# Counters first, x's own sums next, and the small VectorE steps put one at a time behind its additions

## The chip, the cores and the metric

The kernel runs on one core of a Trainium2 chip. The core has TensorE (PE) for matmuls, VectorE (DVE), ScalarE (ACT), GpSimd (POOL) and SyncE (SP), each working through its own queue of instructions in order, and 16 DMA engines that they share. The metric is the device time of one execution in microseconds (us); lower is better. Everything is computed in 32-bit floats.

## The reference

x has 64 batches of 64 tokens with 256 features; each batch has a type from 0 to 2.

```python
# cond: a shared gated layer and one per type, mixed by a gate on the first token
share  = (gelu(x @ sWi0) * (x @ sWi1)) @ sWo
expert = (gelu(x @ Wi0[type]) * (x @ Wi1[type])) @ Wo[type]
w = softmax(relu(concat([expert[:, 0], share[:, 0]]) @ g0) @ g1)
c = expert * w0 + share * w1
x = x + causal_attention(c)              # 16 heads of 16
# cond2: three shared layers and two experts of the type, mixed by a second gate
s_j = relu(x @ share_wi[j]) @ share_wo[j]                 # j = 0, 1, 2
out_a, out_b = the same with expert_wi/expert_wo[type] and [type + 1]
p = softmax(gate_vecs / 0.1)             # weighs the two experts of each type
h = mix of (out_a, out_b, s_0, s_1, s_2) by gate_vecs, gate_w1, gate_w2
# router: three layers, top 2 of 8 experts, capacity 10 per batch and expert
out = x + mixture_of_experts(h)
```

## The kernel before, in words

The kernel keeps nearly everything in one large on-chip tile called `arena`, cut up by hand-written offsets, so most rows of the profile read `arena<-arena`. PSUM banks carry names: `p1c`, `p6c`, `p7c`, `p5c`, `p4c` and `px` belong to cond's shared layer, `sac` and `sbc` to its down projection, names ending in `t` or `d` to cond2's typed and shared layers, `phb`, `plgb` and `pgwb` to cond2's gate.

The 64 batches are worked in 8 blocks of 8 batches (512 tokens). Each large matmul is done by a seven-product scheme (`strassen`, L197): the weight is cut into four blocks a11 to a22 and the tokens into b11 to b22, with sums s1 to s4 of weight blocks (`sum_columns`, L156, and `sum_weights`, L166) and sums t1 to t4 of token blocks (`token_sums`, L179, called by `column_blocks` for x, and again for the hidden layer). Product p6 needs s2 and t2. VectorE adds the products together (L221, L228, L232, L236, L241) between TensorE's matmuls; TensorE can't refill a PSUM bank until the addition that reads it is done. Before the first product, x must be loaded, turned by TensorE (`turn_x`: `px`), copied out of PSUM (L764 on ScalarE, L766 on VectorE) and summed (`cut_x`), and the shared weights must be loaded and summed.

The layers are lists of items; item n has a first part (up projection) and a second part (down projection), and `pipeline` runs the first part of item n+1 before the second part of item n. `hook(item, f)` puts other work between these. `trickle(steps, n)` queues n further small steps of a generator, and `tick()`, called at three places in each up product and three in most down products, runs one of them. The generators are:

- `sort()`: from the batches' types, the sorted place of each batch (`pos_i`) and what derives from it. Its counters come from `iota` (L424: POOL makes an integer ramp, VectorE casts it to float, L428).
- `units()`: per block, which type most of its batches have, and the two places where types meet; 48 operations on up to 24 or 64 columns per partition, in seven steps of several operations each.
- `combine2(s)`: cond2's gate for one block: some small steps (`hidden`, `logits`, `spread`), then eight multiplies of 128x512 (L1072) and six additions (L1316), one per tick.

`masks`, `attention_masks`, `sorted_rows`, `expert_weights` and `small_loads` are one-off preparations, hooked to early items or to cond2.

The order of instructions on each engine is not the order of the source: a scheduler places an instruction as early as its data dependences and its own estimates allow, so small steps gathered in one place of the source can float ahead of the additions around them. `tc.issue_after(ins)` holds the instructions traced inside its block behind `ins` on the engine of `ins`.

Of the kernel before, what the change touches and what calls it, by code (L numbers as in the profile page):

```python
# [82 lines left out]
def adaln_attn_ffn(ctx: ExitStack, tc: tile.TileContext, a: dict, out: bass.AP):  # L83
# [43 lines left out]

    def run(steps):
        for _ in steps:
            pass  # L130
# [25 lines left out]
    def sum_columns(eng, o, fs):  # L156

        a11, a12, a21, a22, s1, s2, s4 = (
            o[b][:, :, fs] for b in ("a11", "a12", "a21", "a22", "s1", "s2", "s4")
        )  # L160
        eng.tensor_add(s1, a21, a22)
        eng.tensor_sub(s2, s1, a11)
        eng.tensor_sub(a21, a11, a21)
        eng.tensor_sub(s4, a12, s2)
# [14 lines left out]
    def token_sums(eng, eng2, b):  # L179
        b11, b12, b21, b22, t1, t2, t3, t4 = (b[n] for n in BLOCKS)  # L180
        eng.tensor_sub(t1, b12, b11)  # L181
        eng.tensor_sub(t2, b22, t1)  # L182
        eng2.tensor_sub(t3, b22, b12)  # L183
        eng2.tensor_sub(t4, b21, t2)  # L184

    def column_blocks(t, at, sums):

        y = {
            f"b{c + 1}{n + 1}": t[:, c, at + n * HB : at + (n + 1) * HB].unsqueeze(1)
            for c in range(2) for n in range(2)  # L190
        }
        for n in range(4):
            y[f"t{n + 1}"] = sums[:, n : n + 1, :]
        token_sums(nc.gpsimd, nc.gpsimd, y)
        return y

    def strassen(name, lhs, rhs, nk, n, width, c_out, c_done, at_st=AT_ST):  # L197
# [23 lines left out]
        nc.vector.tensor_add(u2, wide(x6), s1)  # L221
# [6 lines left out]
        nc.vector.tensor_add(u3, wide(x7), u2)  # L228
# [3 lines left out]
        nc.vector.tensor_add(c_out("22"), wide(x5), u3)  # L232
# [3 lines left out]
        nc.vector.tensor_add(c_out("12"), wide(x5), u2)  # L236
# [4 lines left out]
        nc.vector.tensor_add(c_out("21"), wide(x4), u3)  # L241
# [6 lines left out]
    def trickle(steps, n):  # L248

        between.extend([lambda: next(steps, None)] * n)  # L250

    def tick():
        if between:
            f = between.pop(0)
            if f:
                f()
# [8 lines left out]
    def layer(name, n, ups, down, blocks_of, hops, part, after, ahead=None, at_st=AT_ST, scale=None):  # L265
# [4 lines left out]
        def item(g):  # L270
            def first():
# [31 lines left out]
                token_sums(nc.vector, nc.gpsimd, hb)  # L303
# [120 lines left out]
    def iota(name, shape, pattern, base=0, mult=0, keep=False):  # L424
        ti = tmp(shape, name + "_i").bitcast(I32)
        nc.gpsimd.iota(ti, pattern=pattern, base=base, channel_multiplier=mult)
        tf = const.tile(list(shape), F32, name=name) if keep else tmp(shape, name)
        nc.vector.tensor_copy(tf, ti)  # L428
        return tf

# [72 lines left out]
    def sort():  # L503
        iota18 = iota("iota18", [P, NB], [[1, NB]])
        iota4 = iota("iota4", [P, NB // GB], [[GB, NB // GB]])
        iota_sb = iota("iota_sb", [1, NSTEP, 2], [[SB, NSTEP], [0, 2]]).rearrange("o m b -> o (m b)")
        bvals = iota("bvals", [NB, P], [[0, P]], base=-int(OOB), mult=1)
# [3 lines left out]
        nc.vector.tensor_scalar(oh, iota18[0:NB, 0:NTYPE], typ, None, ALU.is_equal)  # L511
        yield
# [87 lines left out]
    def units():  # L600
        at_tmp[:] = [AT_XE * 256, AT * 256]
# [9 lines left out]
        place = iota("place", [P, NB], [[1, NB]])  # L611
        begin = iota("begin8", [P, NSB], [[NG, NSB]])
        types = iota("types", shape, [[1, NTYPE], [0, NSB]])
        order = iota("order", shape, [[-NSB, NTYPE], [-1, NSB]], base=NTYPE * NSB)
        end = tmp([P, NTYPE], "end")
        nc.vector.tensor_add(end, first, cnt)
        lo, n = tmp(shape, "lo"), tmp(shape, "n")
        for t, of in ((lo, first), (n, end)):
            nc.vector.tensor_tensor(t, by_type(of), by_block(begin), ALU.subtract)
            nc.vector.tensor_scalar(t, t, 0.0, float(NG), ALU.max, ALU.min)  # L620
        nc.vector.tensor_sub(n, n, lo)
        nc.vector.tensor_tensor(lo, lo, by_block(begin), ALU.add)
        yield
        most = tmp([P, NSB], "most")
        nc.vector.tensor_reduce(most, n.rearrange("p t m -> p m t"), AX.X, ALU.max)

        top = tmp(shape, "top")
        nc.vector.tensor_tensor(top, n, by_block(most), ALU.is_equal)
        K.utype = const.tile([P, NSB + NFIX], F32, name="utype")
# [4 lines left out]
        nc.vector.tensor_scalar(none, top[:, 0, :], -1.0, 1.0, ALU.mult, ALU.add)  # L634
        nc.vector.tensor_mul(main, main, none)
        rest = tmp(shape, "rest")
        nc.vector.tensor_tensor(rest, types, by_block(main), ALU.is_equal)
        yield
        nc.vector.tensor_scalar(rest, rest, -1.0, 1.0, ALU.mult, ALU.add)
        nc.vector.tensor_scalar(top, n, 0.0, None, ALU.is_gt)  # L640
        nc.vector.tensor_mul(rest, rest, top)
        yield
        nc.vector.tensor_mul(order, order, rest)
        head = tmp([P, 1], "head")
        flat = "p t m -> p (t m)"
        nc.vector.tensor_reduce(head, order.rearrange(flat), AX.X, ALU.max)
        sel = tmp(shape, "sel")
        nc.vector.tensor_scalar(sel, order, head, None, ALU.is_equal)
        yield
        nc.vector.tensor_mul(sel, sel, rest)  # L650
        begins, sizes = tmp([P, NFIX], "begins"), tmp([P, NFIX], "sizes")
        src = tmp([P, NB], "src")
        nc.vector.tensor_copy(src, place)
        got, inside, by = tmp(shape, "got"), tmp([P, NB], "inside"), tmp([P, 1], "by")
        for j in range(NFIX):
            if j:
                nc.vector.tensor_sub(sel, rest, sel)
            for o, v in (
                (begins[:, j : j + 1], lo), (sizes[:, j : j + 1], n),
                (K.utype[:, NSB + j : NSB + j + 1], types),  # L660
            ):
                nc.vector.tensor_mul(got, sel, v)
                nc.vector.tensor_reduce(o, got.rearrange(flat), AX.X, ALU.add)
            nc.vector.tensor_scalar(inside, place, begins[:, j : j + 1], None, ALU.is_ge)
            nc.vector.tensor_add(by, begins[:, j : j + 1], sizes[:, j : j + 1])
            nc.vector.scalar_tensor_tensor(inside, place, by, inside, ALU.is_lt, ALU.mult)
            nc.vector.tensor_scalar(
                by, begins[:, j : j + 1], -1.0, float(NB + GB * j), ALU.mult, ALU.add
            )
            nc.vector.scalar_tensor_tensor(src, inside, by, src, ALU.mult, ALU.add)  # L670
        K.utype_i = const.tile([1, NSB + NFIX], I32, name="utype_i")
        nc.vector.tensor_copy(K.utype_i, K.utype[0:1, :])
        yield
        nc.vector.tensor_scalar(begins, begins, float(S), None, ALU.mult)
        K.fix_i = const.tile([1, NFIX], I32, name="fix_i")
        nc.vector.tensor_copy(K.fix_i, begins[0:1, :])
        K.src_i = const.tile([1, NB], I32, name="src_i")
        nc.vector.tensor_copy(K.src_i, src[0:1, :])

    def sorted_rows():  # L680

        pm_i = tmp([P, 1], "pm_i").bitcast(I32)
        for r in (0, 64):
            nc.gpsimd.iota(pm_i[r : r + 64, :], pattern=[[0, 1]], base=0, channel_multiplier=1)
        pm = tmp([P, 1], "pm")
        nc.vector.tensor_copy(pm, pm_i)
# [7 lines left out]
        K.erev = iota("erev", [P, E], [[-1, E]], base=E, keep=True)  # L694

        K.slot0 = iota("slot0", [P, NI], [[PAIR, NI]], base=E * SSL, keep=True)
        K.slot0l = iota("slot0l", [P, NI], [[0, NI]], base=E * PAIR, keep=True)
        for t in (K.slot0, K.slot0l):
            nc.vector.tensor_scalar(t[64:128, :], t[64:128, :], float(CAP), None, ALU.add)
# [69 lines left out]
    def cut_x(s):  # L769
        xblocks[s] = column_blocks(xn_of(s), 0, area(AT_XSUM1, 4, HB))  # L770
# [19 lines left out]

    sorting, unit = sort(), units()
    items = []
    for s in range(NSB):
# [6 lines left out]
        if s == 0:  # L800
            hook(its[0], masks, lambda: trickle(sorting, 12))
            hook(its[1], lambda: run(sorting), lambda: sort_x(0), lambda: sort_x(1))
        elif s + 1 < NSB:
            hook(its[0], lambda s=s: sort_x(s + 1))
# [4 lines left out]
    hook(items[2], sorted_rows, lambda: later.update(b=biases()))  # L809
    hook(items[3], lambda: later["b"]())  # L810
    hook(items[4], lambda: trickle(unit, 20))
    hook(items[6], lambda: run(unit), expert_weights)
    hook(items[4], attention_masks)
# [444 lines left out]
    def cut_x1(s, j):  # L1258
        at = AT_XSUM2F if s == 0 and j == 0 else AT_XSUM2[j]
        xblocks["d", s] = column_blocks(X, s * SB, area(at, 4, HB))  # L1260
# [132 lines left out]
    turned = turn_x(0)  # L1393
    cut_x(0)
    with tc.issue_after(turned.ins):
        for o in up1:
            sum_columns(nc.vector, o, slice(0, F // 4))
    for o in up1:
        sum_columns(nc.gpsimd, o, slice(F // 4, F // 2))
    sum_weights(nc.gpsimd, down1)  # L1400
# [36 lines left out]
    for s in range(NSB):  # L1437
        its = shared2(s, 1)
        if s == 0:
            hook(its[0], lambda: load_share(2), small_loads)  # L1440
# [25 lines left out]
    def y_blocks(s):  # L1466
        summed[s] = column_blocks(X, s * SB, area(AT_YSUM[s > 0], 4, HB))
# [67 lines left out]
    for n, _ in enumerate(router(0)):  # L1535
        if n >= 17 and behind:
            f = behind.pop(0)
            if f:
                f()
# [275 lines left out]
```

## Time and profile before

| what | us |
|---|---|
| median of 3 runs | 2874.35 (2872.74 to 2874.54) |
| profiled execution | 2876.09 |
| its span, first to last instruction | 2874.4 |
| TensorE busy in the span | 2817.2 |
| VectorE busy | 1458.5 |
| GpSimd busy | 876.8 |
| ScalarE busy | 835.9 |
| mean granted TensorE clock | 0.992 of full |

The profiled execution is one more execution than the three of the median. In the profile's rows the first two numbers are start and duration, "x4" is the number of instructions merged, and square brackets give the idle time of the engine before the row and what ended it. A row merged of several instructions has the busy time of all of them. In lists of waits, the numbers are the total, the count and the longest. A 32-bit product of two instructions counts as x4 in the trace.

### The profile page before, as it was taken

Reading aid. Unit: us, or ns where it says so; the run is one execution under the profiler, and the core shown is the slowest. Engines: PE = TensorE matmul, PEld = TensorE weight load, DVE = VectorE, ACT = ScalarE, POOL = GpSimd, SP = SyncE. Lnnn points to the kernel's source line nnn. Section 1 sums busy time; section 2 is a strip of 40 time slices with the busy share of each in tenths; the row PEclk is TensorE's granted clock in tenths of the full one; section 3 lists DMA queues with packets and bytes.
Section 4 is the critical chain, followed back from the end, with each engine's and each line's share of the span. In section 5 each row is a group of like instructions: output and inputs, shape, how many; then the busy total and the mean of one; then the engine's idle time right before and its main releaser. Section 6 shows DMA issues by size and latency. Waiting matters only on the chain.

```text
span 2874.4 us, 38591 instructions
## 1 busy us (share of the span) xinstructions
PE 2817.2 (98%) x14137; PEld 2313.5 (80%) x14137; DVE 1458.5 (51%) x2732; ACT 835.9 (29%) x1503; POOL 876.8 (31%) x890
## 2 busy tenths in 40 slices
PE   6999999999999999999999999999999999999998
PEld 5888887777777778888888888888888888887776
DVE  6766515666666675533545566556543333333443
ACT  2122114444444333212222222222222222221333
POOL 4354201111123355522323222225412233223332
PEclk8999999999999999999999999999999999999999
DMA  2354454333341012432333433334300000012330
GB/s 89 108 172 130 138 178 126 110 111 111 111 140 43 34 37 77 139 96 55 133 132 138 145 123 115 131 122 139 112 15 5 6 6 6 6 37 79 91 95 7
DMA packets 221661, 262.29 MB, mean 91 GB/s; under 512 B 106440, under 2 KB 178976, under 8 KB 221344
## 3 DMA queue, kind: packets, MB, share of 16 engines
q1 hardware_dynamic: 205120, 224.62, 25.3%
q0 software_dynamic: 16128, 34.16, 3.5%
q8 instruction: 112, 1.84, 0.3%
q10 hardware_dynamic: 224, 1.05, 0.1%
q14 instruction: 77, 0.63, 0.1%
HBM read 197.79 MB, written 59.35 MB: 89 GB/s over the span
## 4 chain that ended last, share of the span: by engine, by line
PE 88%; DVE 5%; DMA 3%; issue 2%; SPq 1%; POOL 1%; ACT 0%; POOLq 0%; DVEq 0%; ACTq 0%
PE e L115 6%; PE po L115 5%; PE sad L115 5%; PE p5r L115 5%; PE p1r L115 5%; PE peg L115 4%; PE pel L115 4%; PE sbd L115 4%; PE sat L115 3%; PE p5d L115 3%; PE p1d L115 3%; PE p4r L115 2%; PE p6r L115 2%; PE p7r L115 2%; PE sbt L115 2%; PE p5t L115 2%
## 5 line engine op out<-in xcount | busy, mean ns | idle before, releaser
L183 POOL TENSOR_TENSOR arena<-arena 128x512 f32<-128x512 f32 (+1 forms) x152 | 202.5, 1332 | 663.2 <-DVE arena L181 541.2
L184 POOL TENSOR_TENSOR arena<-arena 128x512 f32<-128x512 f32 (+1 forms) x152 | 177.1, 1166 | 17.9 <-DVE arena L182 14.6
L115 PE MATMUL sad<-arena 128*128 128x256 f32 x768 | 175.7, 380 | 0.0
L115 PE MATMUL e<-arena 128*128 128x256 f32 x704 | 173.3, 386 | 0.0
L115 PE MATMUL po<-arena 128*128 128x256 f32 (+1 forms) x704 | 170.3, 399 | 0.1
L1152 POOL TENSOR_TENSOR arena<-arena,vrest 128x256 f32<-128x256 f32 x32 | 24.9, 780 | 456.9 <-ACT arena L1149 456.9
L115 PEld LDWEIGHTS sad<-arena 128*128 128x128 f32 x768 | 144.6, 191 | 19.2
L115 PEld LDWEIGHTS po<-arena 128*128 128x128 f32 x704 | 132.9, 190 | 28.5 <-issue 11.5
L115 PEld LDWEIGHTS e<-arena 128*128 128x128 f32 x704 | 129.3, 190 | 30.4 <-issue 14.8
L115 PE MATMUL p5r<-arena 128*128 128x256 f32 x640 | 151.2, 383 | 0.0
L115 PE MATMUL p1r<-arena 128*128 128x256 f32 x640 | 150.1, 381 | 0.0
L115 PE MATMUL peg<-arena 128*128 128x256 f32 x576 | 138.3, 381 | 0.0
L115 PEld LDWEIGHTS p5r<-arena 128*128 128x128 f32 x640 | 119.2, 190 | 23.4 <-DVE arena L232 7.8
L115 PEld LDWEIGHTS p1r<-arena 128*128 128x128 f32 x640 | 119.7, 190 | 21.6 <-issue 5.9
L115 PE MATMUL pel<-arena 128*128 128x256 f32 x576 | 136.1, 379 | 0.0
L115 PE MATMUL sbd<-arena 128*128 128x256 f32 x576 | 132.2, 379 | 0.0
L294 ACT ACTIVATE arena<-arena 128x512 f32<-128x512 f32 x144 | 90.7, 630 | 117.1 <-DVE arena L232 91.0
L914 DVE TENSOR_TENSOR arena<-pel,arena 128x512 f32<-128x512 f32 x72 | 49.7, 690 | 147.8 <-PE pel L115 146.5
L1646 POOL DMA_INDIRECT xs<-arena,slot_i x64 | 62.6, 979 | 203.0 <-ACT arena L1642 108.5
L115 PEld LDWEIGHTS peg<-arena 128*128 128x128 f32 x576 | 108.4, 190 | 17.1 <-issue 2.3
L115 PEld LDWEIGHTS pel<-arena 128*128 128x128 f32 x576 | 109.4, 190 | 14.9
L115 PEld LDWEIGHTS sbd<-arena 128*128 128x128 f32 x576 | 109.4, 190 | 14.9
(404 smaller groups left out, 5891.9 us busy)
## 6 DMA issues: line engine op xcount, KB each, us to landing
arena<-in_L_cond_Wi SPq DMA_DIRECT2D x72, 512.0 KB
arena<-sums_i SPq DMA_DIRECT2D x32, 896.0 KB
arena<-sums_o SPq DMA_DIRECT2D x32, 896.0 KB
arena<-in_L_cond_Wo SPq DMA_DIRECT2D x36, 512.0 KB
arena<-in_L_ffn_eW SPq DMA_DIRECT2D x16, 1024.0 KB
spill<-arena SPq DMA_DIRECT2D x24, 512.0 KB
arena<-spill POOLq DMA_DIRECT2D x24, 512.0 KB, 5.9
arena<-arena SPq DMA_DIRECT2D x128, 64.0 KB
```

What stands on the lines that cost most here:

```text
L115: nc.tensor.matmul(o, lhsT=lhsT, rhs=rhs, start=start, stop=stop, skip_group_check=shared_bank)
L183: eng2.tensor_sub(t3, b22, b12)
L184: eng2.tensor_sub(t4, b21, t2)
L294: nc.scalar.activation(c_out(ij), src, AF.Relu)
L914: nc.vector.tensor_mul(h, hidden("i1", "pel"), g)
L1152: nc.gpsimd.tensor_mul(vx, vn, K.vrest.rearrange("p a b d -> p (a b d)"))
L1646: nc.gpsimd.indirect_dma_start(out=to.rearrange("e n w -> (e n) w"), out_offset=bass.IndirectOffsetOnAxis(ap=slot_i[:, n, i : i + 1], axis=0),
```

## The change

All iotas and casts move into one function, `counters()`, which runs first, with `masks()`. The first block's x copies and sums are held behind the last cast, and x's first sums move from GpSimd to VectorE; the first weight sums of the two up weights are split over GpSimd (`up1[0]`) and VectorE (`up1[1]`), in the order in which the products need them. `sort`'s ticks start at the first product instead of after the first item. `units()` yields after each operation (48 steps, 70 ticks from item 4 on). A list `opening` always holds the latest VectorE addition of a product and the latest GpSimd sum; every tick, and the preparations wrapped in `behind(...)`, run inside `behind_opening()`, which ties each of their instructions on those engines behind these. cond2's gate goes through the same `tick()` and so is tied too. `expert_weights` and what is left of `units` move from item 6 to item 13.

```diff
+    opening = []
+
+    def behind_opening():
+        st = ExitStack()
+        for ins in opening:
+            st.enter_context(tc.issue_after(ins))
+        return st
...
-    def column_blocks(t, at, sums):
+    def column_blocks(t, at, sums, eng=nc.gpsimd):
...
-        token_sums(nc.gpsimd, nc.gpsimd, y)
-        return y
+        return y, token_sums(eng, eng, y)[1]
...
         product("p6", x6)
-        nc.vector.tensor_add(u2, wide(x6), s1)
+        opening[0:1] = [nc.vector.tensor_add(u2, wide(x6), s1).ins]
...
     def tick():
         if between:
             f = between.pop(0)
             if f:
-                f()
+                with behind_opening():
+                    f()
...
-                token_sums(nc.vector, nc.gpsimd, hb)
+                opening[:] = token_sums(nc.vector, nc.gpsimd, hb)
...
+    def counters():
+        K.iota18 = iota("iota18", [P, NB], [[1, NB]])
...
     def units():
...
         nc.vector.tensor_add(end, first, cnt)
+        yield
...
     def cut_x(s):
-        xblocks[s] = column_blocks(xn_of(s), 0, area(AT_XSUM1, 4, HB))
+        xblocks[s], last = column_blocks(xn_of(s), 0, area(AT_XSUM1, 4, HB), nc.gpsimd if s else nc.vector)
+        return last
...
+    def behind(f):
+        def later():
+            with behind_opening():
+                f()
+        return later
...
         if s == 0:
-            hook(its[0], masks, lambda: trickle(sorting, 12))
-            hook(its[1], lambda: run(sorting), lambda: sort_x(0), lambda: sort_x(1))
+            hook(its[0], behind(lambda: run(sorting)))
+            hook(its[1], lambda: sort_x(0), lambda: sort_x(1))
...
-    hook(items[2], sorted_rows, lambda: later.update(b=biases()))
+    hook(items[2], behind(sorted_rows), lambda: later.update(b=biases()))
...
-    hook(items[4], lambda: trickle(unit, 20))
-    hook(items[6], lambda: run(unit), expert_weights)
-    hook(items[4], attention_masks)
+    hook(items[4], lambda: trickle(unit, 70))
+    hook(items[13], behind(lambda: run(unit)), behind(expert_weights))
+    hook(items[4], behind(attention_masks))
...
-    turned = turn_x(0)
-    cut_x(0)
+    masks()
+    counters()
+    with tc.issue_after(K.cast.ins):
+        turned = turn_x(0)
     with tc.issue_after(turned.ins):
+        cut = cut_x(0)
+    with tc.issue_after(cut):
+        opening.append(sum_columns(nc.vector, up1[1], slice(0, F // 4)).ins)
+    with tc.issue_after(K.iota.ins):
+        r = sum_columns(nc.gpsimd, up1[0], slice(0, F // 4))
+    with tc.issue_after(r.ins):
         for o in up1:
-            sum_columns(nc.vector, o, slice(0, F // 4))
-    for o in up1:
-        sum_columns(nc.gpsimd, o, slice(F // 4, F // 2))
-    sum_weights(nc.gpsimd, down1)
+            sum_columns(nc.gpsimd, o, slice(F // 4, F // 2))
+        opening.append(sum_columns(nc.gpsimd, down1, slice(0, P)).ins)
+    trickle(sorting, 13)
...
-            hook(its[0], lambda: load_share(2), small_loads)
+            hook(its[0], lambda: load_share(2), behind(small_loads))
```

## The prediction

> **What bounds the kernel now.** I read the page's engine rows first, then TensorE's waits, then the timeline of the places where those waits lie. The page gives the bound:
>
> ```profile
> PE 2817.2 (98%) x14137; PEld 2313.5 (80%) x14137; DVE 1458.5 (51%) x2732; ACT 835.9 (29%) x1503; POOL 876.8 (31%) x890
> ```
>
> TensorE is busy for 2817.2 of 2874.4 us, so only 57 us of idle time, plus time spent at a low clock, can be won at all. TensorE's waits, longest first (us in total, times, longest):
>
> ```profile
> PE p6c L115 <- POOL arena L182: 15.6, 2, 14.7
> PE p5t L115 <- DVE arena L232: 6.1, 8, 0.8
> PE px L762 <- DMA arena<-in_x: 5.3, 1, 5.3
> PE p4t L115 <- DVE arena L221: 4.8, 7, 0.7
> ...
> PE p5c L115 <- DVE arena L232: 1.9, 2, 1.5
> PE p7c L115 <- DVE arena L221: 1.8, 1, 1.8
> PE phb L115 <- issue: 1.0, 2, 0.7
> PE p4c L115 <- DVE arena L556: 0.9, 1, 0.9
> ```
>
> The change touches three of these: one wait of 14.7 us at the start (p6c), waits of 4.6 us in x's second block (p5c, p7c, p4c), and fifteen short ones (p5t, p4t) in cond2's typed layer. The start, from the timeline (start, duration):
>
> ```profile
> 10.55 0.72 POOL L161 TENSOR_TENSOR arena<-arena 128x256 f32<-128x256 f32 x1 [7.77 <-DMA arena<-in_L_cond_sWi]
> ...
> 16.60 0.68 DVE L766 COPY arena<-px 128x512 f32<-128x512 f32 x1
> ...
> 18.29 0.94 DVE L163 TENSOR_TENSOR arena<-arena 128x256 f32<-128x256 f32 x1
> ...
> 22.85 0.72 POOL L182 TENSOR_TENSOR arena<-arena 128x256 f32<-128x256 f32 x1
> ```
>
> VectorE copies the second half of the turned x at 16.60, though TensorE finished it at 7.21: the copy stands behind a counter's cast, whose iota POOL makes only at 15.96, behind weight sums. x's sums, on POOL behind more weight sums, end at 23.6, and p6c starts at 23.62.
>
> **x's second block.** On TensorE:
>
> ```profile
> 64.05 1.10 PE L115 MATMUL p4c<-arena 128*128 128x256 f32 x4 [0.93 <-DVE arena L556]
> 66.62 2.02 PE L115 MATMUL p5c<-arena 128*128 128x256 f32 x4 [1.46 <-DVE arena L232]
> 68.43 1.87 PE L115 MATMUL p1c<-arena 128*128 128x256 f32 x4
> ...
> 88.16 1.13 PE L115 MATMUL p7c<-arena 128*128 128x256 f32 x4 [1.81 <-DVE arena L221]
> ```
>
> Between 57.45 and 67.6, and again from 82.66 to 90.4, VectorE runs the small steps of `sort`, `units` and `expert_weights` nearly in a row, ahead of the additions that TensorE needs.
>
> **cond2's gate.** On VectorE, then TensorE:
>
> ```profile
> 1539.89 2.95 DVE L1072 TENSOR_TENSOR arena<-arena,gwab 128x512 f32<-128x512 f32 x3
> ...
> 1545.78 0.68 DVE L221 TENSOR_TENSOR arena<-p6t,arena 128x512 f32<-128x512 f32 x1
> ```
> ```profile
> 1546.51 1.13 PE L115 MATMUL p4t<-arena 128*128 128x256 f32 x4 [0.68 <-DVE arena L221]
> 1548.91 1.13 PE L115 MATMUL p5t<-arena 128*128 128x256 f32 x4 [0.84 <-DVE arena L232]
> ```
>
> Seven bulk steps of the gate precede the addition at 1545.78; p6t, started at 1542.08, was done by 1543.2. The same pair of waits returns every 80 us, in seven blocks.
>
> **The change, part by part.** Where I speak of the changed program I mean the order of its instructions on each engine.
>
> *Counters and x first.* POOL now makes all iotas in a row. Four took 0.59 us at 1.94, three 0.32, two of one column 0.32: thirteen end near 4, before x lands at 5.24. The casts follow by 4.5, so VectorE copies px at 7.25 to 7.9. x's sums go to VectorE (four of 128x256). POOL's first weight sum now takes the pieces that the first product needs; SP's waits date these: the first piece at 6.7, the second at 7.45, then one each 0.76 us, which meets the sixth at 10.48. So s1 runs on POOL from 7.5, and p6c needs s2 (POOL's second) and t2 (VectorE's third).
>
> Here a rule speaks against the change. The row: POOL and VectorE, both adding SBUF to SBUF, took 0.90 and 0.94 at 18.3 to 20.9, with starts 0.87 apart, where alone they take 0.72 and 0.41. The Trainium skill, "SBUF — State Buffer", section "SBUF: two separate sides", says that a VectorE operation with two SBUF inputs and a GpSimd operation that reads SBUF exclude each other for the whole instruction. By the rule each pair costs 0.41+0.72 = 1.13, and t2 is ready at 8.25+0.41+2x1.13 = 10.9; by the row 8.25+0.41+2x0.87 = 10.4; with no contention 9.2. I take the row: p6c at 10.5, that is 13.1 earlier.
>
> The clock: matmuls at 23.62 to 28.9 start 0.43 apart, later 0.215, so twelve at half clock cost 2.6 us. The Trainium skill, "TensorE: Matmul & The Clock Gate", Part 1, says that TensorE is slow after about 3.4 us of idling and full again after about 3.4 us of work. By the rule the work from 5.27 to 8.96 might open the clock before p6c, saving 2.6; by the row (slow until 28.9) nothing is saved. I take nothing: VectorE's four sums of the second weight end at 11.2+4x0.87 = 14.7, and the addition of p6c, the type's one-hot and p_214 queue behind these, so a faster TensorE would only wait there.
>
> *sort in the first block.* About 40 steps of 0.06 to 0.2 us (some 6 us) now lie between 22 additions of 0.60 to 0.69 (14 us), in some 20 us: VectorE is full there. p6 of the first down product waits for t2 by my walk about 0.9 us. I charge 1.0 (0 to 3; steps with two SBUF inputs under POOL's sums took 0.63 to 1.2 at 58 to 62). pos_i is ready at 34.5 instead of 73.9.
>
> *The second block is freed.* Waits 0.93+1.46+1.81+0.19 = 4.4 us go, and p5c and p1c, at 1.66 instead of 0.86 each after these gaps, give 1.6.
>
> *SP and POOL queues.* SP's sixteen sorted copies of x move from 75-112 to 35-72 (2.3 us each), with the first blocks' spills among them; four expert loads follow, landing near 75.5 as they landed 3.7 us after issue. POOL's order is new: expert sums now stand before x's sums of the third block. They start at 75.5, and with four sums (3.6 us), an issue (0.8) and six more (0.72 each) t2 is ready near 85.2, where p6c wants it at 84.3. The trace shows no such row; a free POOL would cost nothing, loads 3 us later 5. I take 1.5. The 0.94 us wait of the same kind at 182 I leave in.
>
> *units, masks, expert_weights.* The 48 units steps go one per tick, to the tenth following item; each takes 0.06 to 0.2 us. Between the additions L228 and L232 VectorE has 0.26 us free, so most cost nothing; a step held by POOL's port costs about 0.4 us. I charge 1.0 (0 to 3). expert_weights moves to item 13 with its Exp, two table loads of 1.28 us on ACT: their cover is the 28 matmuls of a second half (6 us); nothing. The attention masks (about 4 us of POOL) and small_loads (1.5 us, with one 32 KB load behind a memset on SP) go where POOL idles 6 to 12 us at a stretch.
>
> *The gate singly.* Now two bulk multiplies precede L221, one follows it, one lies between L228 and L232, and three additions come behind the chain. From the rows: p7 done +0.27, L228 0.60, one multiply 0.60, so L232 starts 0.34 late and is done 0.06 after the filler matmul (0.43) between p4t and p5t. Each block saves 0.68+0.84-0.06 = 1.46, seven save 10.2 (4 if the slack is not there, 13 if fewer clock drops follow).
>
> Sum: -13.1 +1.0 -4.4 -1.6 +1.5 +1.0 -10.2 = -25.8. The profiled run took 2876.09 (span 2874.40 and 1.69 around it), 1.74 above the median of the three shown: 2876.09-25.8 = 2850.3, against the median **2848.6**.
>
> **Rivals.**
> - *Gate steps just change their place in the wait* (15%): the multiply between L228 and L232 holds p5t in both products of a block by 0.7 us, so 7x1.4 comes back: 2858. For: 0.34 of lateness is certain. Against: the filler.
> - *The opening stays bound by VectorE* (8%): port and small steps keep additions late, half of 13.1 is lost and the second block gains 3 rather than 6: 2858.
> - *POOL takes over* (4%, slower): expert sums ahead of x's sums hold p6c in each later block. It decides once an expert load lands more than about 3 us after 75.5. To end slower, six blocks must lose 5.3 us each (2.7 of wait, 2.6 of half clock behind it): -25.8+31.5 = +5.7, 2880. Against: in the trace POOL idles 12.5 us before an expert load at 164 and TensorE waits only 0.94 for the sums behind it.
> - *The ties hold nothing back*: excluded, as the order does show the steps spread.
>
> **Numbers.** What a measurement of this kernel can tell from no change is about 0.2%, 5.7 us. The forecast's own spread with its bounds has 69%, the two lesser gains 23%; a half of the POOL case gives no change (4%), the whole slower (4%). So faster 0.92, same 0.04, slower 0.04. The range runs from all good ends of the opening, clock and gate (2837) to both lesser gains together (2864).
>
> **What would show it.** Right: p6c starts near 10.5; no p4c or p7c wait on L221, L556 in the second block; the p4t rows gone and p5t below 1 us; the clock's slice at 66-70 full. Wrong: waits of p6c for POOL L192 (x's sums) over 3 us in later blocks; new p5t waits at twice the number; L230 of the first block later than 16.

## The result, and the profile after

The changed kernel takes 2844.85 us (median of 6 runs, 2842.82 to 2849.77), the kernel before 2874.44 in the same set (2872.74 to 2875.54): ratio 0.990, 95% interval 0.9887 to 0.9913. That is 29.6 us less; 25.8 were forecast (2848.6, range 2837 to 2864). The profiled run took 2843.99 with a span of 2842.3, 32.1 less than the profiled run before. The lines moved down in the file: the additions L221, L228, L232, L236, L241 are now L230, L237, L241, L245, L250; x's sums L181 to L184 are L191 to L194.

The page's engine rows, and TensorE's waits (total, count, longest, in us):

```profile
PE 2807.5 (99%) x14137; PEld 2310.1 (81%) x14137; DVE 1507.9 (53%) x2732; ACT 836.7 (29%) x1503; POOL 889.0 (31%) x890
```
```profile
PE px L811 <- DMA arena<-in_x: 6.1, 1, 6.1
...
PE p5c L115 <- DVE arena L241: 2.5, 4, 1.6
PE p6c L115 <- POOL arena L192: 2.4, 2, 1.5
...
PE p5c L115 <- DVE arena L615: 0.7, 1, 0.7
PE sac L115 <- DVE arena L192: 0.6, 1, 0.6
...
PE p5t L115 <- DVE arena L241: 0.2, 1, 0.2
```

The wait of 14.7 us, the p4t row and the waits p7c and p4c are gone; p5t is down from 6.1 to 0.2. New are p6c behind GpSimd's L192 (twice), p5c behind L241 (four times), and two small ones behind sort (L615, and sac). VectorE is busy for 49 us more with the same 2732 instructions. Most of that lies in the gate's own steps: its 48 additions (L1373) take 1172 ns each instead of 682, 64 of its multiplies (L1129) 1013 instead of 798, because some of them now run beside GpSimd's sums (1.76 at 1535.58, beside L193 from 1535.08 to 1536.79).

The opening, from the timeline (start, duration):

```profile
8.09 0.69 DVE L815 COPY arena<-px 128x512 f32<-128x512 f32 x1 [3.48 <-PE px L811]
...
9.92 0.94 DVE L192 TENSOR_TENSOR arena<-arena 128x256 f32<-128x256 f32 x1
...
11.01 2.04 PE L115 MATMUL p6c<-arena 128*128 128x256 f32 x4 [1.06 <-DVE arena L192]
...
15.11 0.68 DVE L230 TENSOR_TENSOR arena<-p6c,arena 128x512 f32<-128x512 f32 x1
```

VectorE's copy now follows the end of px directly, and t2 (L192) releases p6c at 11.01, after the 1.06 us of waiting that remain. In this run x landed at 6.11 instead of 5.27, which is chance (4.96 to 5.48 in all runs below); so places in the first layer are counted from the first px from here on. The first layer as a whole, from the first px to its last p1c, took 320.2 us before and 304.6 after (304.9 in a second profile).

cond2's gate, one block, TensorE only. The first fence is of the kernel before, the second of the changed one:

```profile
1541.21 1.03 PE L115 MATMUL p1t<-arena 128*128 128x256 f32 x4
...
1544.80 1.03 PE L115 MATMUL p5t<-arena 128*128 128x256 f32 x4
1546.51 1.13 PE L115 MATMUL p4t<-arena 128*128 128x256 f32 x4 [0.68 <-DVE arena L221]
1547.48 0.59 PE L115 MATMUL sat<-arena 128*128 128x256 f32 x2
1548.91 1.13 PE L115 MATMUL p5t<-arena 128*128 128x256 f32 x4 [0.84 <-DVE arena L232]
...
1555.49 0.81 PE L115 MATMUL p1t<-arena 128*128 128x256 f32 x3
```
```profile
1525.85 1.03 PE L115 MATMUL p1t<-arena 128*128 128x256 f32 x4
...
1529.44 1.03 PE L115 MATMUL p5t<-arena 128*128 128x256 f32 x4
1530.31 1.03 PE L115 MATMUL p4t<-arena 128*128 128x256 f32 x4
1531.17 0.59 PE L115 MATMUL sat<-arena 128*128 128x256 f32 x2
1531.60 1.12 PE L115 MATMUL p5t<-arena 128*128 128x256 f32 x4
...
1538.17 0.59 PE L115 MATMUL p1t<-arena 128*128 128x256 f32 x2
```

The item that holds the gate took 14.28 us from p1t to p1t and takes 12.32; no wait is printed. The two matmuls of `sat` between p4t and p5t are the prediction's filler.

### The profile page after: what moved, and what is told of

Same layout as the page of the kernel before. It is cut to its first block, busy times and chain, and to the rows that moved or that the text cites. A ratio compares the mean times of both kernels' runs of the same rounds, so it can differ in the third digit from the quotient of the medians.

```text
span 2842.3 us, 38609 instructions
## 1 busy us (share of the span) xinstructions
PE 2807.5 (99%) x14137; PEld 2310.1 (81%) x14137; DVE 1507.9 (53%) x2732; ACT 836.7 (29%) x1503; POOL 889.0 (31%) x890
## 3 DMA queue, kind: packets, MB, share of 16 engines
q8 instruction: 112, 1.84, 0.3%
## 4 chain that ended last, share of the span: by engine, by line
PE 92%; DVE 3%; issue 2%; DMA 1%; SPq 1%; POOL 1%; ACT 0%; POOLq 0%; DVEq 0%; ACTq 0%
PE e L115 6%; PE sad L115 5%; PE po L115 5%; PE p5r L115 5%; PE p1r L115 5%; PE peg L115 4%; PE pel L115 4%; PE sat L115 4%; PE sbd L115 4%; PE p5d L115 3%; PE sbt L115 3%; PE p1d L115 3%; PE p4r L115 2%; PE p6r L115 2%; PE p7r L115 2%; PE p5t L115 2%
## 5 line engine op out<-in xcount | busy, mean ns | idle before, releaser
L193 POOL TENSOR_TENSOR arena<-arena 128x512 f32<-128x512 f32 (+1 forms) x151 | 203.3, 1347 | 711.9 <-DVE arena L191 568.9
L194 POOL TENSOR_TENSOR arena<-arena 128x512 f32<-128x512 f32 (+1 forms) x151 | 183.4, 1215 | 14.3 <-DVE arena L192 10.4
L115 PEld LDWEIGHTS pel<-arena 128*128 128x128 f32 x576 | 109.4, 190 | 14.9
L115 PEld LDWEIGHTS sbd<-arena 128*128 128x128 f32 x576 | 109.4, 190 | 14.9
```

The lines of the kernel that those rows point to most:

```text
L115: nc.tensor.matmul(o, lhsT=lhsT, rhs=rhs, start=start, stop=stop, skip_group_check=shared_bank)
L194: return r.ins, eng2.tensor_sub(t4, b21, t2).ins
```

## The experiments

All were run beside the kernel before. "First layer" is the distance just defined; "gate stage" goes from the first p1t to the last (604.2 before). The last is the noisier. Two profiles of the changed kernel give 588.1 and 593.7 with nearly the same idle time of TensorE (4.2 and 3.9): behind the waits of phb TensorE's clock falls to half in some blocks and not in others, in three stretches of the first profile and six, one of them longer, of the second. Each distance comes from one profiled run, which can lie some us beside its kernel's median.

| kernel | median us | against before in its set | first layer | gate stage |
|---|---|---|---|---|
| changed | 2844.85 | -29.6 | 304.6 | 588.1 |
| changed, again | 2843.45 | -31.5 | 304.9 | 593.7 |
| gate loose | 2859.39 | -13.3 | 305.4 | 600.8 |
| before + gate ties | 2857.84 | -14.9 | 319.2 | 585.0 |
| opening only | 2861.55 | -11.2 | 305.9 | 603.8 |
| ties for the gate only | 2846.10 | -26.6 | 306.4 | 585.0 |
| opening swapped | 2844.98 | -29.4 | 304.8 | 590.8 |
| x sums ahead | 2845.23 | -29.1 | 302.3 | 588.7 |
| units grouped | 2850.86 | -23.5 | 307.9 | 587.9 |
| masks between | 2848.03 | -26.3 | 307.6 | 587.9 |
| sort late, masks between | 2846.31 | -28.6 | 308.4 | 587.4 |
| sort late | 2848.68 | -26.3 | 312.3 | 590.7 |
| no expert sums | 2843.02 | -31.9 | 301.7 | 588.9 |

The intervals are about 0.16% to either side, 4.7 us; where two of these kernels differ by less, I go by the first layer and by rows.

### The gate alone, taken away and added

First in the changed kernel, where `loose` is set at the gate's first block, then in the kernel before, with `opening` as in the change and `gating` set at the same place:

```diff
...
-                with behind_opening():
+                with nullcontext() if loose else behind_opening():
                     f()
```
```diff
...
-                f()
+                with behind_opening() if gating else nullcontext():
+                    f()
```

> The changed kernel (2844.9) with the ties taken off the steps of cond2's gate alone. Theory as predicted: each of seven blocks gives back the idle time of the rows before, 1.46 us, so 10.2: about 2855, p4t and p5t wait 0.68 and 0.84 again. Second theory, after comparing the traces: what counts is the distance from one start to the next, not the idle time in brackets; from p1t of one product to that of the next there were 14.28 us before and 12.33 after, 1.95 more, so 13.7 for seven, and 1 to 3 for clock drops: 2859 to 2862. Rival: the gate's gain came from other ties (units, preparations) or from the clock: about 2845.

> The kernel before (2874.4) with only the ties of cond2's gate added. By the bracketed waits 10.2 less: 2864. By distances from start to start 13.7 to 16 less: 2858 to 2861. Rival, the gate's additions need the other parts of the change: 2874.

Measured: 13.3 less than before instead of 29.6 with the gate loose, and 14.9 less (ratio 0.995, 0.9933 to 0.9967) with its ties alone. The waits of the loose kernel are those of before:

```profile
PE p5t L115 <- DVE arena L241: 6.1, 8, 0.8
...
PE p4t L115 <- DVE arena L230: 4.8, 7, 0.7
```

So the gate's gain stands by itself and needs no other part, and it is nearer 15 than my 10.2. The size comes from the distances: in the kernel before each of the seven items takes 14.28 from p1t to p1t, with the ties alone 12.31, and 7 x 1.97 = 13.8. (The gate stage is 19.3 shorter in this run; most of the rest is half clock, four stretches behind phb before and one here, and these change from run to run.) The brackets add up to only 0.68+0.84 = 1.52 per item. The rest lies in the starts, in the two fences of the section before: p5t to p4t took 1.71 (0.87 undisturbed), p4t to the filler 0.97 (0.86), the filler to p5t 1.43 (0.43), in all 1.95. A bracket counts from the modelled end of the matmul before, 0.16 too late at each wait, and the restarted product runs 0.11 longer.

### The opening alone

No ties; sort, units and the preparations in the groups and places of before:

```diff
-        for ins in opening:
+        for ins in []:
...
-            hook(its[0], behind(lambda: run(sorting)))
-            hook(its[1], lambda: sort_x(0), lambda: sort_x(1))
+            hook(its[0], lambda: trickle(sorting, 13))
+            hook(its[1], lambda: run(sorting), lambda: sort_x(0), lambda: sort_x(1))
```

> Counters first, x's sums on VectorE and the new order of weight sums, as in the changed kernel; sort, units and the preparations in the groups and places of before, and no tie anywhere. As predicted: p6c at 10.5 to 11, 13 us off the kernel before, the second block's waits (4.6 us in brackets, some 6 with the half clock) stay: about 2861. Rival, the opening stays bound by VectorE, as sort's first steps float in among the additions: half of 13 is lost, 2868.

Measured: 11.2 less (0.9963, 0.9949 to 0.9977), as expected at 2861.55. p6c starts 4.35 us behind the first px (4.90 in the changed kernel, 18.35 before), the first layer takes 305.9: 14.3 of the 15.6 that it gains in all. The second block keeps its stalls:

```profile
50.89 1.10 PE L115 MATMUL p4c<-arena 128*128 128x256 f32 x4 [0.93 <-DVE arena L593]
53.47 1.13 PE L115 MATMUL p5c<-arena 128*128 128x256 f32 x4 [1.48 <-DVE arena L241]
72.88 1.13 PE L115 MATMUL p7c<-arena 128*128 128x256 f32 x4 [1.37 <-DVE arena L230]
```

Behind the first two of them TensorE kept its full clock here (p5c 1.13), where the kernel before fell to half behind 0.93 and 1.46 (p5c 2.02).

So sort, units and ties, which take these stalls away, bring only 1.3 us net in this layer. Where the rest of their gain went is the question of the next runs.

### The ties of the first layer

```diff
...
-        for ins in opening:
+        for ins in opening if gating else []:
```

> The changed kernel with all ties off until cond2's gate; order of tracing, single steps and early start of sort stay. Theory: the ties free the second block; without them steps of sort and units gather ahead of additions again and TensorE waits 4 to 8 us more for VectorE in the first three blocks: 2849 to 2853. Rival: the early start and the single steps are enough: 2845, within 1. Second rival: the ties keep steps out of VectorE's idle time and cost something: 2842.

Measured: 2846.10, between theory and first rival; the first layer is 1.8 longer. Without ties the stalls do return, with the half clock behind them (p1c of 1.91 next):

```profile
52.94 1.10 PE L115 MATMUL p4c<-arena 128*128 128x256 f32 x4 [2.20 <-DVE utype_i L728]
55.41 2.07 PE L115 MATMUL p5c<-arena 128*128 128x256 f32 x4 [1.37 <-DVE arena L241]
```

Five waits in the first two blocks sum to 6.3 us, yet the layer is only 1.8 longer. This kernel has none of the changed kernel's new waits, and its first L230 starts 7.4 behind px instead of 9.0. In sum TensorE idles just as long in this layer, 306.40 - 298.64 = 7.8 us against 304.62 - 296.88 = 7.7; the 1.8 is busy time, most of it from matmuls at half clock behind the stalls. So the ties of the first layer move the waits and save next to nothing of them; that they save half clock rests on this one place. In the two kernels without ties in this layer GpSimd's masks had floated into the opening, and VectorE's sums beside these took 0.41 or 0.42 instead of 0.83 to 0.94.

### Masks put there on purpose

```diff
...
     with tc.issue_after(r.ins):
+        attention_masks()
         for o in up1:
```

> The changed kernel with GpSimd's attention masks (memsets and selects, no sums) put between its first four weight sums and the others, instead of in the second block. In the runs with loose ties the masks stood there by themselves, VectorE's sums beside them took 0.41 us instead of 0.83 to 0.94, and the first addition (L230) ran at 12.7 instead of 15.1. Theory, GpSimd's sums hold VectorE's: L230 at about 13 with x landing at 5.3, the second product's p1c (18.95 there, with x landing 0.84 later) at 16 to 17, 1.5 to 2.5 us less: 2843. Rival: only the slower first addition moves, TensorE waits for the second part of the weight sums, which GpSimd now makes 3 us later (p6c at 26): 2845.

The first half of the theory came true: L230 at 12.22, the second product's p1c at 16.09. But the first layer is 3.0 longer (the median 3.2, within the intervals), in a third way that neither named:

```profile
21.52 0.82 DVE L575 TENSOR_TENSOR arena<-arena 128x1 f32<-128x1 f32 x1
22.29 1.26 POOL L173 TENSOR_TENSOR arena<-arena 128x512 f32<-128x512 f32 x1
...
25.55 0.79 PE L115 MATMUL p5c<-arena 128*128 128x256 f32 x1 [2.77 <-DVE arena L241]
```

GpSimd's sums of the down weight, 128x512, now start 3.6 us later behind px, where sort's small steps stand between VectorE's additions. A step on one column (0.15 in the changed kernel) takes 0.8, three of them 1.70, and p5c waits 2.77. What VectorE wins early it loses to the same GpSimd work a little later.

### Which engine sums x

x's first sums on GpSimd, up1[0]'s first weight sums on VectorE:

```diff
-        xblocks[s], last = column_blocks(xn_of(s), 0, area(AT_XSUM1, 4, HB), nc.gpsimd if s else nc.vector)
+        xblocks[s], last = column_blocks(xn_of(s), 0, area(AT_XSUM1, 4, HB))
...
     with tc.issue_after(turned.ins):
-        cut = cut_x(0)
-    with tc.issue_after(cut):
+        r = sum_columns(nc.vector, up1[0], slice(0, F // 4))
+    with tc.issue_after(r.ins):
         opening.append(sum_columns(nc.vector, up1[1], slice(0, F // 4)).ins)
     with tc.issue_after(K.iota.ins):
-        r = sum_columns(nc.gpsimd, up1[0], slice(0, F // 4))
-    with tc.issue_after(r.ins):
+        cut = cut_x(0)
+    with tc.issue_after(cut):
```

> The changed kernel with x's first sums back on GpSimd, and the first weight sums of up1[0], which GpSimd made, on VectorE ahead of those of up1[1]. If the opening's gain comes from the order (counters ahead, the copy of px early) and not from the engine that sums x: p6c within 1 us of the changed kernel's, taken from the end of px (2.1 after it there), and the time 2844 to 2846. If it comes from x's sums being on VectorE: GpSimd's two sums of 0.7 to 0.9 behind the second copy put p6c 1 to 2 us later, 2846 to 2847.

Measured: 2844.98 and 304.8, the same; p6c 4.50 behind the first px against 4.90. (The 2.1 in that text is the changed kernel's distance from the end of the copy, more exactly 2.2; from the end of px it is 3.0.) The opening's gain is the order, counters and copy ahead; the engine makes no difference that can be measured. What the counters, the copy and the order of the weight sums bring singly was not separated.

### x's sums ahead of the hidden sums

```diff
-                opening[:] = token_sums(nc.vector, nc.gpsimd, hb)
                 if g == n - 1 and ahead:
                     ahead()
+                opening[:] = token_sums(nc.vector, nc.gpsimd, hb)
```

> The changed kernel with the next block's x sums traced ahead of the hidden layer's sums. On GpSimd x's t1 and t2 (L191, L192) then stand ahead of the hidden t3 and t4 (L193, L194, 128x512, 1.3 to 1.8 us each). Theory: the two new waits of p6c for L192, 1.54 and 0.87 us and 0.17 more each from start to start, go: 2.7 less, 2842. Rival: the hidden t3 and t4 come later, and p7 or p4 of the down product waits for them instead, or x's copies on VectorE hold L191 and L192 of the hidden layer: 2845, with a new wait of sac or sbc.

In the changed kernel's second block a hidden sum (L193, 128x512) stands between x's t1 and t2 on GpSimd:

```profile
46.00 1.11 POOL L191 TENSOR_TENSOR arena<-arena 128x256 f32<-128x256 f32 x1 [13.22 <-DVE arena L815]
47.07 1.77 POOL L193 TENSOR_TENSOR arena<-arena 128x512 f32<-128x512 f32 x1
48.81 0.71 POOL L192 TENSOR_TENSOR arena<-arena 128x256 f32<-128x256 f32 x1
...
49.58 1.13 PE L115 MATMUL p6c<-arena 128*128 128x256 f32 x4 [1.54 <-POOL arena L192]
```

With the order turned, that wait is gone and no new wait of sac or sbc stands in its place (sac's 0.6 of the first block is there in both kernels); the second, at 86.56, stays at 0.72. The first layer takes 302.3, 2.3 less. The medians do not show it (2845.23 against 2844.85): it is half of their interval.

### GpSimd's expert sums left out

```diff
-        sum_weights(nc.gpsimd, weight_blocks(t, at + 4))
+        nc.gpsimd.memset(area(at + 4, 3 * 256), 0.0)
```

> The changed kernel with GpSimd's sums of the expert weights left out (two in three of its instructions in the first layer; a memset stands in their place, and what they would sum is not computed). Theory: both new costs of the change come from these sums, p6c's waits for L192 (2.4 us) because they stand ahead in GpSimd's queue, and p5c's 1.6 us because they and the hidden sums behind them hold small steps of units on VectorE (L674 took 2.05 us instead of 0.15 to 0.2). Then these waits go, 4 to 5 us with the start-up of TensorE: last p1c, counted from x, at 300, time about 2840. Rival: the hidden layer's own sums (L193, L194) do the holding, and p6c stands behind them too: the waits stay above 1 us each, 2844.

Theory and rival each hold for one of the waits. p6c's 1.54 in the second block stays (the hidden sum); the later one and p5c's 1.61 go, and the first layer takes 301.7 (300 was expected). The step behind p5c's wait, in the changed kernel and then in this one:

```profile
150.03 1.28 POOL L193 TENSOR_TENSOR arena<-arena 128x512 f32<-128x512 f32 x1
150.52 2.05 DVE L674 TENSOR_SCALAR arena<-arena 128x8 f32<-128x8 f32 x1
151.26 1.27 POOL L194 TENSOR_TENSOR arena<-arena 128x512 f32<-128x512 f32 x1
152.48 0.68 DVE L241 TENSOR_TENSOR arena<-p5c,arena 128x512 f32<-128x512 f32 x1
```
```profile
148.99 0.16 DVE L674 TENSOR_SCALAR arena<-arena 128x8 f32<-128x8 f32 x1
149.24 0.69 DVE L241 TENSOR_TENSOR arena<-p5c,arena 128x512 f32<-128x512 f32 x1
```

A step of 8 columns lasts from its start to the end of the second of two GpSimd sums in a row, 2.05 instead of 0.16, and the addition waits behind it. Without the expert sums GpSimd's two hidden sums come at another time and the step is free.

### Single steps of units

The yields that the change added to units() are taken out again, so that it runs in its seven groups of before, each group in one tick and still tied. The first of them:

```diff
         nc.vector.tensor_add(end, first, cnt)
-        yield
         lo, n = tmp(shape, "lo"), tmp(shape, "n")
         for t, of in ((lo, first), (n, end)):
             nc.vector.tensor_tensor(t, by_type(of), by_block(begin), ALU.subtract)
-            yield
             nc.vector.tensor_scalar(t, t, 0.0, float(NG), ALU.max, ALU.min)
-            yield
```

> The changed kernel with units() in its seven groups of before, each group in one tick, still tied behind VectorE's additions. If it is the single steps that keep the additions in time: groups of 5 to 24 steps of 0.06 to 0.2 us stand together ahead of an addition, p5c or p4c wait 1 to 3 us in two or three places, 2847 to 2850. Rival, each small step on its own can be caught behind a GpSimd sum (the wait of 1.61 us at 153 stands behind one that took 2.05 us), so fewer places are better: 2842 to 2844.

2850.86 and a first layer of 307.9, 3.3 longer, as the first theory has it. (The run in the trace was the fastest of four, 2845.10.) Four waits stand between 133 and 152: p5c 1.43, p4c 0.62, p5c 1.18, p1c 0.84. So the single steps matter; each may be caught by a GpSimd sum, but a group ahead of an addition is worse.

### A version meant to beat both

x's sums ahead as above, and sort later; one of the two also has the masks in the opening:

```diff
...
+    between.extend([None] * 7)
     trickle(sorting, 13)
...
-            hook(its[0], behind(lambda: run(sorting)))
-            hook(its[1], lambda: sort_x(0), lambda: sort_x(1))
+            hook(its[1], behind(lambda: run(sorting)), lambda: sort_x(0), lambda: sort_x(1))
```

> A version meant to beat both: next block's x sums ahead of the hidden ones, the masks between GpSimd's first weight sums and the others, and sort's ticks seven later (its rest one item later), so that its small steps come behind GpSimd's weight sums, which held them for 0.8 to 1.7 us where only the masks were moved. Theory that GpSimd's sums hold VectorE's instructions: opening 2 us earlier, no wait of 2.8 in the first block, x sums 2.3: the last p1c of the first layer, counted from the landing of x, at 300 to 302 instead of 304.6, and 2840 to 2842. Rival: sort's steps only collect ahead of the second block's additions again and 1 to 3 us of waits for L230 or L237 come back there: 2843 to 2846.

> The same as the version meant to beat both, but with the masks left where the changed kernel has them. The opening then keeps its first addition at 15 (x at 6.1), so the last p1c, counted from x, comes 1 to 2 us later than there, 302 to 303.5; 2841 to 2844. Rival: the masks cost as much in the opening as they bring: the same as there.

> The changed kernel itself, beside the three others of this set on the same chip. 2843 to 2847, some 29 us below the kernel before; p6c waits for GpSimd's L192 twice (1.5 and 0.5 to 0.9 us) and p5c once more than 1 us for L241.

Neither beats the changed kernel of the same set (2843.45): 2846.31 and 2848.68, and the rival was right. In the first block no wait is left behind p6c, but sort's rest stands ahead of the second block, with L613 and L606 (0.15 elsewhere) at 1.2 each beside GpSimd, and the clock falls (with the masks):

```profile
48.21 0.40 PE L115 MATMUL p_sort<-arena,ones 64*128 64x64 f32 x2 [1.92 <-DVE arena L618]
...
50.04 2.08 PE L115 MATMUL p1c<-arena 128*128 128x256 f32 x4 [1.20 <-ACT arena L226]
51.90 1.91 PE L115 MATMUL p7c<-arena 128*128 128x256 f32 x4
```

A wait of p6c for L192 (2.28) at 130.86, again with half clock behind it, adds to that. Of all versions that compute everything none is measurably better than the changed kernel; x's sums ahead is better by rows.

## Why the prediction was right, point by point

**The opening (-13.1).** Right, by its own steps. p6c came 4.90 behind px where 10.5 - 5.24 = 5.26 was taken. The 8.25 from which that sum counts is derived nowhere; from the copy's end at 7.9 the same terms, 0.41+2x0.87, give 10.05, which is 4.8 behind px. L230 came 9.0 behind px where the sum had 9.4. The pairs of VectorE and GpSimd sums started 0.86 to 0.87 apart, as the row of before said, not 1.13. The clock was undecided: p6c ran at half pace (2.04) in both profiles of the changed kernel and in three others, at full (1.10) in four more, all the same up to there. (The pace is read from the durations; the profile's clock reads 1.00 from 6 to 17 all the same.) The step that a faster TensorE would only wait there held: with p6c at full pace p_214 (`p` in the rows) waits 1.92 to 2.05 for L547 in three runs, with p6c at half pace 0.39 and 0.40. First the changed kernel, then x sums ahead:

```profile
16.62 0.35 PE L115 MATMUL p<-arena,ones 64*128 64x3 f32 x2 [0.39 <-DVE arena L547]
```
```profile
10.76 1.10 PE L115 MATMUL p6c<-arena 128*128 128x256 f32 x4 [1.86 <-DVE arena L192]
...
16.37 0.35 PE L115 MATMUL p<-arena,ones 64*128 64x3 f32 x2 [1.92 <-DVE arena L547]
```

**sort in the first block (+1.0).** 0.59 (sac) and 0.70 (p5c, where sort's L611 took 1.26 beside a GpSimd sum, L194), with the start-up about 1.6. Both are absent where sort comes later.

**The second block (-4.4 and -1.6).** All four waits are gone; the clock between 57 and 75 is 1.00 instead of 0.91, 18 x 0.09 = 1.6. Before and after (the first number behind the comma is TensorE's busy time, the third from the end the clock):

```profile
57.00:75.00 18.00, 15.61 (x63) 12.33 (x62) 15.66 (x65) 3.66 (x6) 4.94 (x5) 0.91 0.00 1
```
```profile
57.00:75.00 18.00, 18.00 (x86) 15.15 (x85) 14.31 (x25) 2.79 (x6) 2.54 (x2) 1.00 0.34 82
```

**GpSimd's order (+1.5).** Mis-sized and half mis-placed. The third block's wait was seen and measured 0.87 (0.50 in the second profile). The second block's 1.54 was not: I had followed the expert sums and not the hidden sum L193 between x's t1 and t2. Together about 2.7 from start to start. That the third block's wait came at the forecast 0.9 is luck: 75.5+3.6+0.8+6x0.72 is 84.2, not 85.2, and by that nothing would have waited. On the chip the sums began later, and five of GpSimd's sums there took 1.16 or 1.17 instead of 0.72 (from 80.70 to 87.16), which the sum did not have.

**Single steps of units (+1.0).** Mis-sized. I let a caught step cost 0.4; L674 took 2.05 and cost TensorE 1.61, a second wait 0.31.

**The wait at 182 that I left in** went, about 1 us. These errors cancel: the first layer was forecast at -15.6 and gave 320.2 - 304.6 = 15.6. By stages, counted from the first px: the first `sbc` came at 50.5 before and at 38.3 after, 12.2 earlier (12.1 in the sum); the third, ahead of the third block's first product, at 96.6 and 78.0, 18.6 earlier (18.1); the layer's last at 336.4 and 320.8, 15.6 earlier. So the second block gained 6.4, and without the 1.7 of the wait that was not seen it would have been some 8, where its brackets and clock made 6.0. Behind it 3.0 was lost where 2.5 was charged. That the whole agrees to a tenth is luck.

**The gate (-10.2).** Right in mechanism and in the place of every step: two multiplies ahead of the first addition, one between L230 and L237, one ahead of L241, and the filler covers the lateness. Wrong in size: the term "0.68+0.84-0.06 = 1.46" per block measured 1.97, because it took the bracket for the time lost. That is 13.8 in distances, and 14.9 alone on the chip; the surplus of 3.6 over 10.2 is most of the 3.8 us by which the whole came out better. (Eight bulk steps stood ahead of the addition at 1545.78, not seven.)

**The rivals.** That the gate's steps only move fell: p5t waits 0.2 once, not twice per block. That the opening stays bound by VectorE fell. GpSimd did not take over: p6c's longest wait for it was 1.54, under the 3 that were named, and in no block but two. Two sums of this part are off without consequence: six times 5.3 is 31.8, not 31.5, and both lesser gains together make about 2867 by their own terms, not the 2864 of the range.

## What to carry to other kernels

Price a wait that is to go by the distance between the same two starts with and without it, not by the idle time printed beside it; here that was 1.97 against 1.52 for a pair. When small steps are spread between the additions of a full engine, look at what the other engine on the same memory does at that moment: a step of 0.16 us can take as long as the sum, or the two sums, that hold it. And when an engine is relieved early, ask which of its later work now meets what was shifted; moved masks and later sort both lost again what they had gained.

## What the runs showed of the hardware that was not expected

- VectorE's small steps that read and write on-chip memory can be held by GpSimd through two of its sums in a row (0.16 to 2.05 us for 8 columns, also 1.61 and 1.84 in other runs), while its additions that read PSUM kept 0.68 or 0.69 beside GpSimd's sums (L230 at 15.11). The Trainium skill, "SBUF — State Buffer", section "SBUF: two separate sides", says that the loser of the shared ports blocks for the whole instruction. The held steps block at least that long, though one that started within the first sum (150.52) ended only with the second, at 152.57; the 128x256 pairs (0.87 apart, 0.41 and 0.72 alone) are shorter than that rule makes them; and beside GpSimd's small selects, which read on-chip memory too, VectorE's sums kept 0.41 (with masks between, 10.76 beside 10.52 to 11.23).
- TensorE's clock can fall to half behind gaps shorter than the about 3.4 us of idling that the Trainium skill, "TensorE: Matmul & The Clock Gate", Part 1, gives: behind one of 2.28 us, one of 2.77, and 1.92 and 1.20 within 2 us. Single gaps of 1.54, 1.61 and 2.09 left it full. No threshold comes out of these runs: 0.93 and 1.46 in a row gave half clock before, 0.93 and 1.48 full clock with the opening alone; a gap of 2.05 ahead of p_214 gave half clock (gate loose), one of 2.04 at the same place did not (units grouped); and in cond2's gate a wait of 0.35 with the 1.92 us of phb's small matmuls (128x8) behind it was followed by half clock at 1816.5, one of 0.43 with the same matmuls at 1736.3 was not.
